# Two pieces of the last batch's rows with three feed-forward pieces, and VectorE and ScalarE bound to the written order in a transformer decoder layer

## The chip, the core and the metric

The kernel runs on one core of a Trainium2 chip. The metric is the device time of one execution in microseconds (us), as the median of three runs. Beside these there is one profiled execution, whose trace is read here. The engines are TensorE (PE; its weight loads are PEld), VectorE (DVE), ScalarE (ACT), GpSimd (POOL) and SyncE (SP), which here issues DMAs.

## The reference

The kernel computes one pre-LayerNorm decoder layer in float32 on x of shape (4, 1024, 256), with a context of shape (4, 64, 256). There are 16 heads of width 16. Cut to what matters:

```python
def layernorm(x): return (x - mean(x)) / sqrt(var(x) + 1e-5)

# self-attention: the energies are not scaled, the softmax is divided by sqrt(256)
q, k, v = split(layernorm(x) @ W_qkv + b_qkv)
attn = softmax(einsum('bqhe,bkhe->bqhk', q, k)) / sqrt(256)
x = x + einsum('bihv,bvhd->bihd', attn, v).reshape(x.shape) @ W_out + b_out

# cross-attention to 64 context tokens for each batch
q = layernorm(x) @ Wq.T + bq; k = ctx @ Wk.T + bk; v = ctx @ Wv.T + bv
x = x + softmax(q k / sqrt(16)) v @ Wo.T + bo

# feed-forward, 256 -> 1024 -> 256; absmean makes ternary weights (-1, 0, 1)
h = gelu(layernorm(x) @ absmean(W_fc).T)            # exact gelu
h = layernorm(h) * ln_w + ln_b
x = x + h @ absmean(W_proj).T
```

`absmean(W)` divides W by the mean of its absolute values, rounds, and clips to one.

## The kernel before, in words

**Phases.** A prologue (to about 66 us) normalises batch 0 and projects its first q and k. The attention loop (66 to 1114 us) follows, then the tail: the last batch's output rows beside the feed-forward of all batches (to 1273 us), and feed-forward alone to the end.

**Attention loop.** There are 16 units: four batches (`b`) of four head groups (`g`), a group being four heads in two pairs. A unit has 16 steps: two halves of 512 query tokens by eight blocks of 128 key tokens. "Step 8.3" here means step 3 of unit 8. A step does the scores of the first pair of heads (`scores`, exponentials on line 848, two tiles of 128x512 on ScalarE), then pieces of other work, then the scores of the second pair, more pieces, and last `weigh`, which multiplies the step before's exponentials by the values on TensorE.

Scores are computed twice. One unit ahead, `maxima` computes them with queries as rows, so that VectorE can reduce each row to its maximum (line 424, two reduces of 128x512 for each pair of score tiles). After the 16 pairs of tiles of a half, lines 430 to 434 negate the maxima and split them into a high and a low part (`nm`, `nm_s`), and lines 436 to 439 turn them with eight small transposes (`mT`). When the unit is reached, a matmul with the selector `sel` adds the negated maxima to the scores in PSUM, so that ScalarE takes the exponential straight from there. The generator `maxima` yields after each pair of tiles, after `nm` and after the turn: 18 yields for half a unit. The loop takes one after the first scores of a step, one after the second, and one more at every fourth step.

**Work between the scores.** Other work is written as generators, cut into pieces at each `yield`: `ln1` (LayerNorm and transposes for the next batch), `project` (q and k, stored to DRAM in `kept_q` and `kept_k`), `values`, `context` (keys and values of the context, lines 444 to 530), `post` (a batch's output projection, second LayerNorm, cross-attention and third statistics, lines 532 to 628), `ternary` (the feed-forward weights) and `bias_row`. They stand in three queues (class `Line`): `due`, `later` and `aside`. Each step adds to a queue's `credit` its pieces left over the steps left to `end`. `fill` (lines 668 to 686) first takes one piece with the tag "free" (it needs no PSUM) from each queue, and then up to `n` pieces of the kind asked for, "rows" (transposes and small work) or "cols" (projections), from the queue with the most credit. The `urgent` queue holds `finish`, which turns and normalises a half's attention output.

A LayerNorm's statistics are `bn_stats` and `bn_aggr` (lines 234 and 235) for each block of 128 tokens. Its reciprocal deviation is a Sqrt on ScalarE (line 240) and a reciprocal on VectorE (line 241); I call these two, with the table loads around the Sqrt, an *rstd group*. The rows are normalised on VectorE (`xn`, line 246) and turned on TensorE (line 60). Right after, GpSimd adds a bias row to the x that was read (`add_row`, line 270). `x_kept` holds a batch's x in DRAM between its attention and its feed-forward.

**What sets the order.** `ordered = tc.keep_in_program_order` pins an instruction to the order in which it is written, among the pinned ones of its engine. TensorE (lines 57 and 60) and the DMAs of SyncE (line 63) are pinned. VectorE, ScalarE and GpSimd are left to a scheduler, which gives each engine its order when the program is built. On the chip each engine runs its own instructions in that order and waits on semaphores for the others. PSUM has one bank for the weighed values (`ps_acc`) and a ring of seven (`ps_ring`) for everything else, so a bank that VectorE or ScalarE has not read yet holds TensorE up.

**Tail.** The feed-forward works on eight halves of batches (512 tokens each). `widen(i)` normalises a half (xn; `xh` and the rest `xl`, lines 259 and 261), multiplies by `wfc` (16 matmuls for each of the four token blocks), takes Gelu (line 955) and statistics of h (lines 958 and 959), then the rstd group, `nmr` (line 963), and normalises h, two blocks on VectorE (line 966) and two on ScalarE (line 969). `narrow(i)` turns h, splits it into `hT` and `hl` (lines 989 and 990), multiplies by `wproj` and adds to x. The places in `WIDE` and `NARROW` give the order of the two. While the last batch's `post` lasts (74 pieces) they alternate with it, decided by `turn`:

```python
    while tag is not None or narrows:
        turn += 1
        if tag is not None and turn % 2:
            exps += "Exp" in tag
            tag = next(last, None)
            continue
```

Of the kernel before, what the change touches and what calls it, by code (L numbers as in the profile page):

```python
# [30 lines left out]
def decoder_layer(ctx, tc, a, out):  # L31
# [21 lines left out]

    ordered = tc.keep_in_program_order
# [7 lines left out]
    def dma(**kwargs):  # L62
        ordered(nc.sync.dma_start(**kwargs))

# [65 lines left out]
    nc.vector.memset(eps_t, LN_EPS)  # L130
# [99 lines left out]
    def ln_stats(pool, mv, blocks):  # L230

        for i, t in blocks:
            st = pool.tile([P, 6], F32, tag="bn", name="bn", bufs=3)
            nc.vector.bn_stats(out=st, in_=xs(t)[:, 0, :])  # L234
            nc.vector.bn_aggr(out=mv[:, i, :], in_=st)

    def ln_rstd(pool, rs, mv):
        n = mv.shape[1]
        sd = pool.tile([P, n], F32, tag="sd", name="sd", bufs=2)
        nc.scalar.activation(sd, mv[:, :, 1], AF.Sqrt, bias=eps_t[:, 0:1])  # L240
        nc.vector.reciprocal(out=rs, in_=sd)

    def ln_normalised(pool, mv, rs, i, t, n):
        xn = pool.tile([P, n, E], F32, tag="xn", name="xn", bufs=2)
        for k in range(n):
            nc.vector.tensor_scalar(  # L246
                xn[:, k, :], xs(t + k)[:, 0, :], mv[:, i + k, 0:1], rs[:, i + k : i + k + 1],
                ALU.subtract, ALU.mult,
            )
        return xn  # L250

    def ln_transposed(dst, xn, rest=None):

        def copy(tokens, r, sides, v):
            to = of_side(dst[:, :, tokens], r, sides)
            nc.scalar.copy(to, v)
            if rest is not None:  # L260
                nc.vector.tensor_tensor(  # L261
                    of_side(rest[:, :, tokens], r, sides), v, to.bitcast(F32), ALU.subtract
                )

        turned_tokens(copy, lambda c, k: xn[:, k, c * P : (c + 1) * P], xn.shape[1])
# [9 lines left out]
    def head_proj(dst, w, bias, g, src, cols):  # L275
        pq = bank()[:, 0 : cols.stop - cols.start]
        product(pq, [(w[:, c, g * P : (g + 1) * P], src[:, c, cols]) for c in range(2)])
        nc.scalar.activation(dst[:, cols], pq, AF.Identity, bias=bias[:, g : g + 1])

    def normalised(dst, acc_sb):  # L280


        views = turned([acc_sb[:, n * P : (n + 1) * P] for n in range(4)])
        n = NG // len(views)
        for side, v in enumerate(views):
            heads = v.rearrange("p t (j e) -> p t j e", e=32)
            r = post_pool.tile([P, 4, n, 1], F32, tag="r", name="r", bufs=3)
            nc.vector.reciprocal(out=r, in_=heads[:, :, :, 0:1])
            nc.vector.tensor_tensor(
                dst[:, :, side * n : (side + 1) * n, :], heads[:, :, :, 1 : 1 + D],  # L290
                r.to_broadcast([P, 4, n, D]), ALU.mult,
            )

    def transposed_blocks(src, n):
        t = post_pool.tile([P, 2, n * P], F32, tag="ao", name="ao")
        turned_tokens(
            lambda tokens, r, sides, v: nc.scalar.copy(of_side(t[:, :, tokens], r, sides), v), src, n
        )
        return t

    def out_proj(ao, k, n, w, t):

        py = bank()
        for i in range(n):
            cols = slice((k + i) * P, (k + i + 1) * P)
            product(py[:, i * E : (i + 1) * E], [(ao[:, c, cols], w[:, c, :]) for c in range(2)])
        nc.vector.tensor_tensor(
            xs(t, n), xs(t, n), py[:, 0 : n * E].rearrange("p (n d) -> p n d", n=n), ALU.add
        )
# [23 lines left out]
    def project(b, c):  # L333
# [6 lines left out]
        for side, half in ((0, 0), (1, 0), (1, 1), (0, 1)):  # L340
# [3 lines left out]
            for i0 in range(0, 512, width):  # L344
# [6 lines left out]
                nc.scalar.activation(hl[:, 0, part].bitcast(F32R), pq, AF.Identity, bias=bias)  # L351
                nc.vector.scalar_tensor_tensor(
# [40 lines left out]
    def values(b):  # L393
        for i in range(NT):
# [4 lines left out]
            nc.vector.tensor_tensor(  # L399
# [4 lines left out]
    def maxima(u):  # L404

        mx = main.tile([P, NT, NG, 2], F32, tag="mx", name="mx", bufs=2)
        m_of[u] = []
        for half in range(2):
# [4 lines left out]
            for t, pair in order:  # L413
                q, k = qk_of[u][pair]
                for kh in range(2):
# [7 lines left out]
                    for n, pm in enumerate(sides):  # L423
                        nc.vector.tensor_reduce(  # L424
                            mx[:, t, 2 * pair + n : 2 * pair + n + 1, kh], pm, AX.X, ALU.max
                        )
                    yield
            sl = slice(half * 4, half * 4 + 4)
            nm = main.tile([P, 4, NG], F32, tag="nm", name="nm", bufs=2)
            nc.vector.tensor_reduce(nm, mx[:, sl, :, :], AX.X, ALU.max, negate=True)  # L430
            by_side = nm.rearrange("p t (a n) -> p t n a", a=2)
            dst = nm_s[:, :, :, 0:2, :]
            nc.vector.tensor_copy(dst[:, :, :, :, 0].bitcast(F32R), by_side)
            nc.vector.tensor_tensor(dst[:, :, :, :, 1], by_side, dst[:, :, :, :, 0], ALU.subtract)
            yield
            views = turned([nm_s[:, n, :, :, :].rearrange("p n a l -> p (n a l)") for n in range(4)])
            mT = main.tile([P, 512], F32R, tag="mT", name="mT", bufs=3)
            for r, v in enumerate(views):
                nc.scalar.copy(mT.rearrange("p (k r i) -> p r k i", r=len(views), k=4)[:, r, :, :], v)  # L439
            m_of[u].append(mT)  # L440
            yield
# [26 lines left out]
    def context():  # L468
# [9 lines left out]
        nc.vector.tensor_reduce(own, ident.rearrange("p (s j i) -> p j s i", s=2, j=4), AX.XY, ALU.add)  # L478
        one = post_pool.tile([P, 32], F32, tag="one", name="one")
        nc.vector.tensor_reduce(one, ident.rearrange("p (s h l) -> p h s l", s=2, l=2), AX.XY, ALU.add)  # L480
        nc.vector.tensor_copy(
            sel_x, one[:, 0:8].rearrange("p (h o) -> p h o", o=1).to_broadcast([P, 8, SK])
        )
        for c in range(2):
# [5 lines left out]
            for j in range(4):  # L490
                nc.vector.tensor_scalar(
# [3 lines left out]
        for b in range(B):  # L495
# [9 lines left out]
            for n in range(2):  # L505
                r = slice(64 * n, 64 * n + 64)
                nc.vector.tensor_tensor(
# [8 lines left out]
    def post(b):  # L516
# [23 lines left out]
        for half in range(2):  # L540
# [14 lines left out]
            for t in range(4):  # L555
# [9 lines left out]
                for s in range(2):  # L565
                    nc.vector.tensor_reduce(  # L566
# [5 lines left out]
            nc.vector.tensor_copy(dst[:, :, :, :, 0].bitcast(F32R), nm)  # L572
            nc.vector.tensor_tensor(dst[:, :, :, :, 1], nm, dst[:, :, :, :, 0], ALU.subtract)
# [3 lines left out]
            for r, v in enumerate(views):  # L577
                nc.scalar.copy(mT.rearrange("p (k r i) -> p r k i", r=len(views), k=4)[:, r, :, :], v)
            att = post_pool.tile([P, 4, NG, NG * D], F32, tag="attx", name="attx")
            before = None  # L580
            for g in range(NG):
# [16 lines left out]
                for p in range(2):  # L598
                    nc.scalar.activation(ex[:, p, :], pe[p], AF.Exp, scale=0.25)
# [11 lines left out]
                nc.scalar.copy(oT, pa)  # L611
# [56 lines left out]
    def fill(kind, n):  # L668

        slots[0] += 1  # L670
        for line in (due, later, aside):
            if line.work and "free" in line.tag and (line is not aside or line.credit >= 1.0):
                line.step(line is aside)
        for least in (0.5, 1.25)[:n]:
# [20 lines left out]
    def ternary(name, *shape):  # L695
# [13 lines left out]
        for i, cols in enumerate(parts):  # L709
            yield "free"  # L710
            nc.vector.tensor_reduce(
# [3 lines left out]
        nc.vector.memset(ones, 1.0)  # L715
# [4 lines left out]
        nc.vector.tensor_reduce(thr[:, 0:1], pt[:, 0 : len(parts)], AX.X, ALU.add)  # L720
        nc.vector.tensor_scalar(thr[:, 0:1], thr[:, 0:1], 1.0 / (P * n), GAMMA_EPS, ALU.mult, ALU.add)
        nc.vector.tensor_scalar(thr[:, 1:2], thr[:, 0:1], -0.5, None, ALU.mult)
        nc.vector.tensor_scalar(thr[:, 0:1], thr[:, 0:1], 0.5, None, ALU.mult)
        for cols in parts:
            yield "free"
            neg = main.tile([P, 512], F32, tag="hl", name="neg", bufs=2)
            nc.vector.tensor_scalar(neg, flat[:, cols], thr[:, 1:2], None, ALU.is_lt)
            nc.vector.scalar_tensor_tensor(
# [4 lines left out]
    def bias_row():  # L733
# [10 lines left out]
        nc.vector.tensor_copy(yrow, pt[:, 0:E])  # L744
# [22 lines left out]
    def weigh(u, half, kb, exps, acc):  # L767
# [11 lines left out]
        nc.scalar.copy(oT, acc)  # L779
# [27 lines left out]
    for pair in range(2):  # L807

        for n in range(2):
            c = 64 * n + 2 * pair  # L810
            for i in range(2):
                nc.vector.tensor_tensor(
                    sel_f[:, pair, :], sel_f[:, pair, :], ident[:, c + i : c + i + 1].to_broadcast([P, P]), ALU.add
                )
    nc.vector.tensor_copy(sel, sel_f)
    add_row(0, bo, NT)
    tops = (None for u in range(NU) for _ in maxima(u))
# [4 lines left out]
    for i in range(18):  # L822
        next(tops)
        if i % 3 != 0 and i < 15:
            due.step()
    due.credit = 0.0
# [5 lines left out]
    def scores(u, half, kb, pair):  # L832
# [14 lines left out]
        for n in range(2):  # L847
            nc.scalar.activation(ex[:, n, :], pe[n], AF.Exp)  # L848
        return ex

    for u in range(NU):
        b, g = divmod(u, NG)
        due.end = later.end = aside.end = 2 * NT * NG * (b + 1)
# [23 lines left out]
        for step in range(2 * NT):  # L877
# [12 lines left out]
            next(tops, None)  # L890
            if urgent:
                fill("rows", 0)
# [5 lines left out]
            for _ in range(1 + (step % 4 == 3) + (u == 0 and step < 3)):  # L898
                next(tops, None)
# [11 lines left out]
    weigh(*pending, acc)  # L911
    while urgent:
# [17 lines left out]
    def widen(i):  # L930
# [14 lines left out]
        for t in range(NH):  # L945
# [9 lines left out]
            nc.scalar.activation(h[:, t, :], ph.rearrange("p a f -> p (a f)"), AF.Gelu)  # L955
            st = ffn.tile([P, 2, 6], F32, tag="bnh", name="bnh", bufs=3)
            for half in range(2):
                nc.vector.bn_stats(out=st[:, half, :], in_=h[:, t, half * 512 : (half + 1) * 512])  # L958
            nc.vector.bn_aggr(out=mv[:, t, :], in_=st)
# [3 lines left out]
        nc.vector.scalar_tensor_tensor(nmr, mv[:, :, 0], -1.0, rs, ALU.mult, ALU.mult)  # L963
        for t in range(0, NH, 2):
            yield ""
            nc.vector.tensor_scalar(
                h[:, t, :], h[:, t, :], mv[:, t, 0:1], rs[:, t : t + 1], ALU.subtract, ALU.mult
            )
            nc.scalar.activation(  # L969
                h[:, t + 1, :], h[:, t + 1, :], AF.Identity, bias=nmr[:, t + 1 : t + 2],  # L970
                scale=rs[:, t + 1 : t + 2],
            )

    def narrow(i):
# [6 lines left out]
        for c in range(HID // P + 2):  # L981
            if c < HID // P:
# [6 lines left out]
                nc.scalar.activation(hT, pt, AF.Copy, scale=w)  # L989
                nc.vector.scalar_tensor_tensor(hl, pt, w, hT.bitcast(F32), ALU.mult, ALU.subtract)  # L990
# [13 lines left out]
        for n in range(2):  # L1004
            rows = xs(t0 + 2 * n, 2)
            nc.vector.tensor_tensor(
# [22 lines left out]

    WIDE, NARROW = (-6, -4, 0, 1, 3, 7, 8, 10, 12), (2, 4, 5, 6, 9, 11, 13, 14, 15)  # L1030
# [5 lines left out]
    while tag is not None or narrows:  # L1036
        turn += 1
        if tag is not None and turn % 2:
# [78 lines left out]
```

## Time and profile before

| | |
|---|---|
| median of three runs | 1395.13 us (1393.49 to 1396.28) |
| the profiled execution, its own time | 1396.0 us |
| its span (first to last instruction) | 1394.2 us, 1.8 us less |
| TensorE busy | 1292.1 us, 93% of the span, 10984 matmuls |
| VectorE busy | 1048.5 us, 75%, 2177 instructions |
| ScalarE busy | 864.0 us, 62%, 1573 instructions |
| GpSimd busy | 81.6 us, 6% |
| mean clock granted to TensorE | 0.964 of full speed |

The reduces of line 424 are VectorE's largest group (639.5 us, 1024 of them), the exponentials of line 848 ScalarE's (544.5 us, 1024 of them). Weighing is the largest part of TensorE's work (279.6 us).

How to read it: a row of the timeline or of the groups has the start and the duration in us, the engine, the line of the kernel, the operation, the tile it writes and the tiles it reads, their shapes, and a count. Square brackets hold the engine's idle time just before and what ended it: `[6.77 <-POOL xwk L452]` says that the engine stood for 6.77 us until GpSimd's instruction of line 452 on tile xwk was done. A busy time counts from an instruction's start to its end, so a TensorE that runs at half clock, or waits inside a chain of matmuls, still counts as busy.

### The profile page before, as it was taken

To read this page: it belongs to the slowest core of one execution; us is meant where nothing else is said; L and a number is where in the kernel's file an instruction comes from. 1 tells how busy PE (TensorE), PEld (TensorE's weight loads), DVE (VectorE), ACT (ScalarE), POOL (GpSimd) and SP (SyncE) were. 2 spreads that over 40 slices of the span, in tenths; PEclk is the share of its full clock that TensorE was granted. 3 is DMA by queue.
4 is the path that set the end of the run, shared out by engine and by line. 5 is a ranking of instruction groups with operands and counts; after the bars stand their busy time and mean duration, and the time that the engine had idled before them with its cause. 6 is when DMAs were issued, how large, how long until landed. Compare 5 with 4: busy or idle time off the path is not lost.

```text
span 1394.2 us, 27597 instructions
## 1 busy us (share of the span) xinstructions
PE 1292.1 (93%) x10984; PEld 721.6 (52%) x10984; DVE 1048.5 (75%) x2177; ACT 864.0 (62%) x1573; POOL 81.6 (6%) x86
## 2 busy tenths in 40 slices
PE   3779999999999999989999999999999989998877
PEld 1334544545454554444545544544445466676767
DVE  5798877777877887788878777878888266565655
ACT  1156666756667677666676676666666846556554
POOL 5021000000100000011000000010000021000100
PEclk9789999999999999989999999999999999999989
DMA  5450312302020211211111202221300010010000
GB/s 155 120 157 31 107 42 81 92 32 77 31 77 1 62 33 29 74 49 41 52 55 38 62 1 86 67 77 46 87 6 1 2 61 1 16 46 16 16 31 31
DMA packets 45841, 72.85 MB, mean 52 GB/s; under 512 B 11025, under 2 KB 27665, under 8 KB 45713
## 3 DMA queue, kind: packets, MB, share of 16 engines
q1 hardware_dynamic: 44448, 68.47, 16.6%
q8 instruction: 87, 1.43, 0.4%
q10 hardware_dynamic: 1072, 2.10, 0.4%
q0 software_dynamic: 192, 0.52, 0.2%
q14 instruction: 42, 0.34, 0.1%
HBM read 46.94 MB, written 24.12 MB: 51 GB/s over the span
## 4 chain that ended last, share of the span: by engine, by line
PE 76%; DVE 16%; ACT 3%; DMA 3%; issue 1%; POOL 1%; SPq 0%; DVEq 0%; POOLq 0%; ACTq 0%
PE ps_ring L57 44%; PE ps_acc L57 16%; PE ps_wide L57 8%; DVE mx L424 8%; PE ps_misc L57 3%; PE ps_ring L60 2%; DVE xn L246 2%; PE ps_misc L60 2%; DMA x<-in_x 1%; DVE nm L566 1%; DVE bn L234 1%; ACT h L955 1%; DMA wk_in<-in_wk 1%; ACT h L969 1%; DVE hl L990 1%
## 5 line engine op out<-in xcount | busy, mean ns | idle before, releaser
L424 DVE TENSOR_REDUCE mx<-ps_ring 128x1 f32<-128x512 f32 x1024 | 639.5, 680 | 117.5 <-PE ps_ring L57 116.5
L848 ACT ACTIVATE exp<-ps_ring 128x512 f32<-128x512 f32 x1024 | 544.5, 603 | 234.7 <-PE ps_ring L57 230.9
L57 PE MATMUL ps_ring<-k,q 64*128 64x512 f32 x1024 | 264.7, 434 | 18.4 <-DMA k<-kept_k 10.9
L57 PE MATMUL ps_acc<-exp,v_sb 128*32 128x512 f32 x2048 | 279.6, 619 | 0.0
L57 PE MATMUL ps_ring<-q,k 64*128 64x512 f32 x1024 | 271.9, 476 | 5.5 <-ACT exp L848 2.6
L57 PE MATMUL ps_ring<-mT,sel 64*128 64x512 f32 x1024 | 227.9, 403 | 0.2 <-ACT mT L439 0.2
L57 PEld LDWEIGHTS ps_ring<-q,k 64*128 64x128 f32 x1024 | 112.2, 187 | 194.5 <-issue 61.2
L57 PEld LDWEIGHTS ps_ring<-k,q 64*128 64x128 f32 x1024 | 126.7, 188 | 106.6 <-ACT exp L848 45.2
L57 PEld LDWEIGHTS ps_ring<-mT,sel 64*128 64x128 f32 x1024 | 107.2, 189 | 6.9 <-ACT mT L439 0.7
L57 PEld LDWEIGHTS ps_acc<-exp,v_sb 128*32 128x32 f32 x2048 | 40.8, 109 | 62.6 <-issue 56.0
L958 DVE BATCH_NORM_STATS2 bnh<-h 128x6 f32<-128x512 f32 x64 | 41.3, 681 | 39.3 <-ACT h L955 39.3
L955 ACT ACTIVATE h<-ps_wide 128x1024 f32<-128x1024 f32 x32 | 32.8, 1026 | 57.6 <-PE ps_wide L57 57.6
L57 PE MATMUL ps_wide<-wproj,hl 128*128 128x256 f32 x256 | 46.8, 306 | 18.4 <-DVE hl L990 18.4
L57 PE MATMUL ps_wide<-wfc,xl 128*128 128x512 f32 x128 | 57.0, 445 | 4.8 <-DVE xl L261 3.3
L246 DVE TENSOR_SCALAR xn<-x,mv,rs 128x256 f32<-128x256 f32 x96 | 55.4, 631 | 6.6 <-PE ps_misc L60 5.6
L990 DVE SCALAR_TENSOR_TENSOR hl<-ps_misc,lnw,hT 128x512 fp32r<-128x512 f32 x64 | 46.3, 730 | 16.9 <-ACT hT L989 16.9
L270 POOL TENSOR_TENSOR x<-x,xbo 128x512 f32<-128x512 f32 x16 | 21.3, 1330 | 559.6 <-DVE xn L246 304.5
L57 PE MATMUL ps_wide<-wfc,xh 128*128 128x512 f32 x128 | 53.7, 420 | 0.0
L989 ACT ACTIVATE hT<-ps_misc,lnw 128x512 fp32r<-128x512 f32 x64 | 42.8, 688 | 16.8 <-PE ps_misc L60 16.8
L351 ACT ACTIVATE hl<-ps_ring,bq_c 128x256 fp32r<-128x256 f32 (+1 forms) x30 | 14.7, 490 | 54.8 <-PE ps_ring L57 50.5
L57 PEld LDWEIGHTS ps_wide<-wproj,hl 128*128 128x128 f32 x256 | 35.3, 194 | 23.6 <-DVE hl L990 20.9
L234 DVE BATCH_NORM_STATS2 bn<-x 128x6 f32<-128x256 f32 x96 | 38.9, 416 | 10.2 <-DMA x<-in_x 8.6
(161 smaller groups left out, 1452.2 us busy)
## 6 DMA issues: line engine op xcount, KB each, us to landing
k<-kept_k SPq DMA_DIRECT2D x248, 64.0 KB
q<-kept_q SPq DMA_DIRECT2D x240, 64.0 KB
kept_q<-hl SPq DMA_DIRECT2D x15, 512.0 KB
kept_k<-hl SPq DMA_DIRECT2D x14, 512.0 KB
out<-x SPq DMA_DIRECT2D x16, 256.0 KB
x<-in_x SPq DMA_DIRECT2D x3, 1024.0 KB
x_kept<-x SPq DMA_DIRECT2D x3, 1024.0 KB
x<-x_kept SPq DMA_DIRECT2D x3, 1024.0 KB
```

The source lines that it names most:

```text
L57: ordered(nc.tensor.matmul(*args, **kwargs))
L60: ordered(nc.tensor.transpose(*args))
L234: nc.vector.bn_stats(out=st, in_=xs(t)[:, 0, :])
L246: nc.vector.tensor_scalar(xn[:, k, :], xs(t + k)[:, 0, :], mv[:, i + k, 0:1], rs[:, i + k : i + k + 1], ALU.subtract, ALU.mult,)
L270: nc.gpsimd.tensor_tensor(xs(t, 2), xs(t, 2), row.rearrange("p (o d) -> p o d", o=1).to_broadcast([P, 2, E]), ALU.add,)
L351: nc.scalar.activation(hl[:, 0, part].bitcast(F32R), pq, AF.Identity, bias=bias)
L424: nc.vector.tensor_reduce(mx[:, t, 2 * pair + n : 2 * pair + n + 1, kh], pm, AX.X, ALU.max)
L848: nc.scalar.activation(ex[:, n, :], pe[n], AF.Exp)
L955: nc.scalar.activation(h[:, t, :], ph.rearrange("p a f -> p (a f)"), AF.Gelu)
L958: nc.vector.bn_stats(out=st[:, half, :], in_=h[:, t, half * 512 : (half + 1) * 512])
L989: nc.scalar.activation(hT, pt, AF.Copy, scale=w)
L990: nc.vector.scalar_tensor_tensor(hl, pt, w, hT.bitcast(F32), ALU.mult, ALU.subtract)
```

## The change

It has six parts.

1. A thin wrapper `Engine` around VectorE and ScalarE pins every instruction while its flag `fixed` is set. The flag is set from the attention loop's first scores until after its last `weigh`, so there both engines run in the written order.
2. In the tail, single instructions are pinned: the copy to `xh` and the subtraction for `xl`, the pair that normalises h, and the pair `hT` and `hl`. The rest of the tail stays with the scheduler.
3. The end of `maxima` becomes a generator of its own, `turn_maxima`. The loop now takes two pairs of maxima every step, none at a fourth place; `nm` is written right after a half's last pair, and the turn takes the next step's "rows" slot, where `urgent` work otherwise stands. In those two cases a "rows" piece may still go first, if `later` has a credit of 1.5 (`behind`).
4. The queue `later` ends two steps sooner.
5. In `fill`, a queue that has given a free piece counts as having been served in this slot.
6. In the tail, of five turns two go to `post` and three to the feed-forward, where they took one each.

```diff
+    class Engine:
+        def __init__(self, engine):
+            self.engine, self.fixed = engine, False
+        def __getattr__(self, name):
+            op = getattr(self.engine, name)
+            def call(*args, **kwargs):
+                done = op(*args, **kwargs)
+                if self.fixed:
+                    ordered(done)
+                return done
+            return call
+    vector, scalar = Engine(nc.vector), Engine(nc.scalar)
...
     def maxima(u):
...
+                    if kh == 1 and (t, pair) == order[-1]:
+                        turning.append(turn_maxima(u, mx[:, half * 4 : half * 4 + 4, :, :]))
                     yield
-            sl = slice(half * 4, half * 4 + 4)
-            nm = main.tile([P, 4, NG], F32, tag="nm", name="nm", bufs=2)
...
+    def turn_maxima(u, mx):
+        nm = main.tile([P, 4, NG], F32, tag="nm", name="nm", bufs=2)
+        vector.tensor_reduce(nm, mx, AX.X, ALU.max, negate=True)
...
             if line.work and "free" in line.tag and (line is not aside or line.credit >= 1.0):
                 line.step(line is aside)
+                line.slot = slots[0]
...
+    def top():
+        next(tops, None)
+        if turning and turning[-1] not in begun:
+            next(turning[-1])
+            begun[turning[-1]] = slots[0]
...
-    for i in range(18):
-        next(tops)
+    for i in range(16):
+        top()
...
+    run(turning.popleft())
...
+    vector.fixed = scalar.fixed = True
     for u in range(NU):
         b, g = divmod(u, NG)
-        due.end = later.end = aside.end = 2 * NT * NG * (b + 1)
+        due.end = aside.end = 2 * NT * NG * (b + 1)
+        later.end = due.end - 2
...
             exps = [scores(u, half, kb, 0)]
-            next(tops, None)
-            if urgent:
-                fill("rows", 0)
+            top()
+            behind = 1 if later.credit >= 1.5 else 0
+            if turning and begun[turning[0]] < slots[0]:
+                fill("rows", behind)
+                run(turning.popleft())
+            elif urgent:
+                fill("rows", behind)
                 urgent.popleft()()
             else:
                 fill("rows", 1)
             exps.append(scores(u, half, kb, 1))
-            for _ in range(1 + (step % 4 == 3) + (u == 0 and step < 3)):
-                next(tops, None)
+            for _ in range(2 if u == 0 and step < 3 else 1):
+                top()
...
     weigh(*pending, acc)
+    vector.fixed = scalar.fixed = False
...
-            nc.scalar.copy(to, v)
+            copied = scalar.copy(to, v)
             if rest is not None:
-                nc.vector.tensor_tensor(
+                ordered(copied)
+                ordered(vector.tensor_tensor(
                     of_side(rest[:, :, tokens], r, sides), v, to.bitcast(F32), ALU.subtract
...
-        if tag is not None and turn % 2:
+        if tag is not None and turn % 5 in (0, 2):
             exps += "Exp" in tag
             tag = next(last, None)
             continue
```

The pinned pairs for h and for `hT` and `hl` are written as that for `xh` and `xl`.

## Prediction

> **What bounds it now.** I read the page first: engines' busy time, then the chain that ended last.
>
> ```profile
> PE 1292.1 (93%) x10984; PEld 721.6 (52%) x10984; DVE 1048.5 (75%) x2177; ACT 864.0 (62%) x1573; POOL 81.6 (6%) x86
> PE 76%; DVE 16%; ACT 3%; DMA 3%; issue 1%; POOL 1%; SPq 0%; DVEq 0%; POOLq 0%; ACTq 0%
> ```
>
> TensorE bounds; a gain can only be a wait of TensorE that goes. Next the table by stretches (start:end, length, busy PE, PEld, DVE, ACT, POOL, granted clock): attention loop, FFN beside the last `post`, FFN alone, then two pairs inside one tail round.
>
> ```profile
> 65.90:1113.70 1047.80, 1014.16 (x9207) 512.91 (x9208) 829.11 (x1732) 697.59 (x1351) 36.11 (x41) 0.98 0.19 54
> 1123.00:1273.00 150.00, 137.72 (x800) 100.62 (x800) 95.09 (x203) 87.33 (x119) 18.21 (x14) 0.97 0.09 27
> 1273.00:1394.20 121.20, 97.57 (x632) 87.62 (x632) 75.87 (x139) 67.28 (x85) 6.62 (x5) 0.91 0.07 22
> 1328.90:1334.00 5.10, 5.06 (x16) 4.38 (x17) 1.28 (x2) 0.51 (x1) 0.00 (x0) 0.51 0.25 84
> 1334.00:1345.00 11.00, 11.00 (x72) 9.53 (x71) 7.43 (x14) 6.19 (x8) 0.00 (x0) 1.00 0.03 10
> 1353.90:1358.00 4.10, 4.10 (x15) 3.57 (x16) 1.28 (x2) 0.45 (x1) 0.00 (x0) 0.58 0.18 57
> ```
>
> A busy PE hides stalls, so I priced the loop by steps from the timeline (time between successive first exps). A bare step (eight score matmuls, two pairs of maxima, a weighing) takes 2.9 us; a piece of eight projection matmuls adds 0.87; a piece of transposes 0.52; `kx,q` 0.82, `mTx` 0.77, `ex,vx` 0.97. For 255 steps: 255x2.9 + 154x0.87 + 116x0.52 + 24x0.82 + 24x0.77 + 12x0.97 = 984. They took 1045.7, so 61 us is excess: unit 0 15.3, unit 4 5.8, unit 8 17.2, unit 12 8.7, units 13 to 15 11.2, the rest 3. That is what the loop can lose. Unit 0's, in the timeline:
>
> ```profile
> 93.08 5.52 DVE L246 TENSOR_SCALAR xn<-x,mv,rs 128x256 f32<-128x256 f32 x8
> 98.68 1.26 POOL L270 TENSOR_TENSOR x<-x,bo 128x512 f32<-128x512 f32 x1 [0.23 <-DVE xn L246]
> 99.89 1.48 POOL L452 COPY xwk<-xwk_in 128x64 f32<-128x64 f32 x8
> 100.18 2.10 PE L57 MATMUL ps_ring<-ctx_in,xwk 128*32 128x256 f32 x16 [6.77 <-POOL xwk L452]
> ```
>
> GpSimd did batch 1's `bo` adds (they wait on xn) ahead of casting xwk, and TensorE stood 6.77 us. Unit 8 has a load instead, and each of the loop's eight rstd groups takes ScalarE from the exps:
>
> ```profile
> 586.02 0.39 SPq L63 DMA_DIRECT2D x<-in_x  x1
> 592.16 0.75 DVE L234 BATCH_NORM_STATS2 bn<-x 128x6 f32<-128x256 f32 x2 [0.23 <-DMA x<-in_x]
> 375.98 1.28 ACT L240 ACT_TABLE_LOAD   x1
> 377.27 0.30 ACT L240 ACTIVATE sd<-mv,eps_t 128x8 f32<-128x8 f32 x1
> 377.59 1.28 ACT L848 ACT_TABLE_LOAD   x1
> ```
>
> Last, the chain through one round of the FFN-only tail (start, us, piece); the next half's xn stand ahead of this half's rstd and normalising on VectorE:
>
> ```profile
> 1321.50 2.27 DVE xn L246 x4
> 1323.77 0.10 DVE rsh L241
> 1323.89 1.25 DVE nmr L963
> 1325.16 2.37 ACT h L969 x2
> 1327.53 0.58 ACT hT L989
> 1328.14 0.76 DVE hl L990
> 1328.94 3.36 PE ps_wide L57 x11
> ```
>
> TensorE waits 5.3 us from 1323.6 to 1328.9, then runs 5.1 us at clock 0.51: 2.5 us more.
>
> **Loop: what the order changes.** The two programs' written orders, compared by engine, show that nearly everything reading PSUM already ran in it: 63 of 1445 VectorE and 35 of 1340 ScalarE instructions of the loop come later than written. So binding moves mainly what reads no PSUM: statistics, Sqrt and its two table loads, reciprocals, xn. The groups move from steps (unit.step) 0.6, 4.12, 8.0, 8.3, 8.12, 12.0 and 12.12 to 2.12 (batch 1's ln1 comes off unit 0), 4.14, 8.0, 8.2, 8.14, 12.0 and 12.14, and one Sqrt at 0.10 stands where the scheduler had shared a load: table loads go from 42 to 43.
>
> Unit 0: on GpSimd the casts now come before the `bo` adds, so the 6.8 us wait goes, and about 3 us of the half-clock time behind it. The rstd group pushed into unit 2 costs there what the groups at 4.12, 8.12 and 12.12 cost: excesses of 5.7, 5.1, 5.2. By hand, in the new order, such a group costs 0.65 + 0.75 ahead of it and about 3.0 held by Sqrt (1.28 + 0.30 + 1.28 above): 4.4 to 4.7. Net -6.8 - 3 + 4.7 = **-5**; bounds: -10 (the new group hidden) to 0 (late next are the casts' own loads: xwq's cast at 102.4 us still waited 1.03 for its DMA). Those three groups: 3x(4.7 - 5.7) = **-3**, bounds -9 to +9.
>
> Unit ends 8 and 12: VectorE must now do a block's statistics (0.39 + 0.16 = 0.56 each, six of them 3.4 us) and the rstd ahead of the reduces that free the ring's banks; queued behind are the maxima, and TensorE waits for their bank. At 8.0 the statistics also wait for the load: issued at 586.0, landed 592.1, needed 2 to 4.4 us earlier in the new order. About 15 against 12 us at unit 8, 5 against 3.5 at 12: **+4.5**, bounds -2 to +16 (load wait and statistics fully exposed, both ends). SP is pinned in both programs, so the x_kept store (581.6 to 586.0) and this load keep their places.
>
> Ternary pieces (units 13 to 15): their 0.5-and-over VectorE work falls behind a step's reduces, not between them, and a line waits a slot after a free piece: 11.2 to about 6, **-5**, bounds -9 to +4. Maxima: two pairs each step in place of a third one every fourth step; a pair adds 0.51 of TensorE and 1.23 of VectorE and the count is the same (992 matmuls), nm and turn a slot apart: **0**, bounds -5 to +5; cover is that VectorE has 0.79 of the loop's time, and without it each of 32 turns would add up to 0.5. `later.end - 2`: three xwo pieces move from behind the loop into it, 3x0.87 = 2.6 and back: 0. Engine wrapper: 0. Loop **-8.5**.
>
> **Tail.** The ratio of post to FFN pieces goes from 1:1 to 2:3, post's 74 pieces last longer, and when they end 22 of 32 widening groups and 32 of 64 narrowing groups are out, not 16 and 24. A bare round took 27.3 us (1295.7, 1323.0, 1350.3) for 19.2 of TensorE's own; one with post beside it loses nothing like 8. So 1 to 1.5 rounds less of 5.3 + 2.5: 1.25x7.8 = **-10**, bounds -16 to 0. Post's first 33 us (1123 on) hold 10 us of waits for att, wo and xn; three FFN pieces between cover some: **-4**, bounds -10 to +4 (more post latency at the end). The pinned xh/xl, h and hT/hl pairs already run in that order but for 7 hl: 0. One more table load, 1.28: **+1.3**. Tail **-12.7**.
>
> On the clock: the rows show 0.51 after a wait of 5.3 us and 0.58 after one of about 3.2, and I assume that the rounds which stay bare keep both. [...]
>
> On the loads: the rows show the Sqrt at 377.27, 0.01 us after its load ended, so I take 1.28 a load. [...]
>
> **Sum.** 1396.0 (span 1394.2 + 1.8) - 8.5 - 12.7 = 1374.8; the median of the runs shown stands 0.9 below the profiled execution: **1374**. The terms' half-widths, 5, 9, 9, 6.5, 5, 8 and 7, taken as independent, make 19; four fifths of that, 16 each way, is this case's own range: 1358 to 1390.
>
> **Rivals.** (1) *Slower: blocked queues.* Eight groups, forecast near 5 each, expose all: 4x1.12 of statistics, 2.9 of Sqrt and loads, 2.6 of half clock = 10. Full price 8x5 = +40: 1414; the sign turns where eight groups eat the 21.2 (2.65 each) and the 2.8 of a visible loss (0.35): 3 us more per group, 8 in all. So 1398 to 1414. For: an in-order queue holds exps behind a Sqrt that waits for statistics. Against: before already runs those pieces between exps at about 5. Chance 0.20. (2) *Loop unmoved*, only the tail gains: 1382; for, the 63 and 35 above. 0.13. (3) *Most excess goes*, 61 to 25, tail -15: 1344; for, scheduler-placed pieces lie in most of it. 0.15. (4) *Nothing moves*, both orders end equal: 1395. 0.06. Forecast 0.46.
>
> **Chances.** 0.2% (2.8 us) is what a measurement of this kernel can tell. Faster: 0.46 + 0.13 + 0.15 less 0.03 for the forecast's edge: 0.71; same 0.09; slower 0.20. The range leaves out about 0.1 on each side: below 1350 two thirds of rival 3, above 1406 half of rival 1.
>
> **To look for.** In after: no wait of 6.8 on xwk near 100 us; unit 2 longer by 4 to 5 and unit 0 shorter by 10; unit 8's end near 15; VectorE's reduces late by at most 1.2 per statistics piece; three bare rounds or fewer in the tail. Wrong if the loop's excess is above 65, or the tail from the loop's end is not shorter by 8.

## The result and the profile after

The changed kernel takes 1419.32 us (1413.62 to 1420.83, four runs) against 1395.51 for the kernel before in the same comparison: 23.8 us slower, a ratio of 1.0165 with a 95% interval of 1.0134 to 1.0197. The forecast was 1374, its own range 1358 to 1390; the chances were reckoned with limits of 1350 and 1406. The measured time lies above all of them.

I cut each profiled execution into three: up to the first exp of the loop; the loop, from there to the first exp of its last step; and the tail, from there to the end.

| kernel | span | first exp at | loop | tail | median of its runs |
|---|---|---|---|---|---|
| before | 1394.2 | 65.9 | 1045.7 | 282.6 | 1395.5 |
| after | 1418.8 | 64.5 | 1067.9 | 286.4 | 1419.3 |

So the loop lost 22.2 us and the tail 3.8. By the prediction's step prices the loop's own work is 2.6 more (three xwo pieces moved in) and its excess over them rose from about 61 to about 81. Both signs of being wrong that the prediction named have come: an excess above 65, and a tail that is not 8 shorter.

The page of the changed kernel, engines and chain. TensorE's line 57 is now 58, SyncE's 63 is 64, and everything that goes through the wrapper has line 76:

```profile
PE 1307.1 (92%) x10984; PEld 729.6 (51%) x10984; DVE 1060.2 (75%) x2177; ACT 865.6 (61%) x1574; POOL 80.8 (6%) x86
PE 68%; DVE 20%; ACT 5%; DMA 3%; SPq 2%; issue 1%; POOL 1%; DVEq 0%; ACTq 0%; POOLq 0%
```

The same instructions ran (one more on ScalarE, the table load), but TensorE's share of the chain fell from 76% to 68%, and VectorE, ScalarE and SyncE's queue took it over. The table by stretches (loop, feed-forward beside `post`, feed-forward alone; columns as in the prediction):

```profile
64.50:1134.50 1070.00, 1031.48 (x9252) 519.88 (x9254) 842.07 (x1736) 697.67 (x1351) 35.69 (x41) 0.97 0.19 54
1143.70:1333.70 190.00, 167.08 (x952) 128.26 (x953) 116.17 (x236) 107.21 (x141) 18.46 (x14) 0.93 0.06 20
1333.70:1418.80 85.10, 69.32 (x481) 62.90 (x479) 56.71 (x103) 48.99 (x63) 5.21 (x4) 0.95 0.08 26
```

The stretch beside `post` grew by 40 us and the bare one shrank by 36, as the ratio is meant to do. The clock beside `post` fell from 0.97 to 0.93, though, which speaks for waits in it that were not there (behind the one of 6.26 us shown below it was 0.50, from 1245.2 to 1250). Now the loop's places. Unit 0, from the timeline:

```profile
93.47 0.38 SPq L64 DMA_DIRECT2D kept_k<-hl  x1
96.26 0.47 ACT L76 ACTIVATE hl<-ps_ring,bq_c 128x256 fp32r<-128x256 f32 x1 [8.85 <-DMA kept_k<-hl]
96.63 2.05 ACT L76 ACTIVATE exp<-ps_ring 128x512 f32<-128x512 f32 x4
97.28 0.97 PE L58 MATMUL ps_ring<-k,q 64*128 64x512 f32 x2 [7.56 <-ACT exp L76]
99.88 1.93 PE L58 MATMUL ps_ring<-ctx_in,xwk 128*32 128x256 f32 x16
```

The last line has no bracket any more: the wait for xwk is gone, as forecast. But three lines up ScalarE stands 8.85 us before a copy into an `hl` tile, whose buffer a store of k is still to read. That store was issued only at 93.47, behind fetches of q and k and small loads that had kept SyncE's queue busy since 62. The exps are ready behind the copy: TensorE had done their scores by 89.72 (97.28 less the 7.56 it then stands for them). They start at 96.63, behind it, and that the copy is first comes from the binding. The end of unit 7 and the start of unit 8:

```profile
587.09 1.28 ACT L76 ACT_TABLE_LOAD   x1
588.08 0.42 DVE L76 BATCH_NORM_STATS2 bn<-x 128x6 f32<-128x256 f32 x1
591.16 0.39 SPq L64 DMA_DIRECT2D x<-in_x  x1
591.39 0.30 ACT L76 ACTIVATE sd<-mv,eps_t 128x8 f32<-128x8 f32 x1 [3.01 <-DVE mv L76]
591.71 1.28 ACT L76 ACT_TABLE_LOAD   x1
592.53 0.79 PE L58 MATMUL ps_ring<-k,q 64*128 64x512 f32 x1 [3.82 <-DVE mx L76]
593.00 2.06 ACT L76 ACTIVATE exp<-ps_ring 128x512 f32<-128x512 f32 x4
597.25 0.43 DVE L76 BATCH_NORM_STATS2 bn<-x 128x6 f32<-128x256 f32 x1 [4.17 <-DMA x<-in_x]
```

`flush` wrote the batch's last three statistics pieces in one row. VectorE does them ahead of the reduces, from 588.08 to 591.35; ScalarE has loaded the Sqrt's table and waits 3.01 us for them, and TensorE waits 3.82 for a bank. Then VectorE stands 4.17 us for a load of x with reduces ready behind it. Unit 13 shows the same with the raw weights:

```profile
965.18 0.69 DVE L76 TENSOR_REDUCE part<-raw 128x1 f32<-128x512 f32 x1 [3.56 <-DMA raw<-in_wfc]
968.61 1.09 ACT L76 ACTIVATE exp<-ps_ring 128x512 f32<-128x512 f32 x2 [3.93 <-PE ps_ring L58]
```

Behind the waits of units 0, 7 and 8 TensorE runs at a granted clock of 0.50 to 0.60 (the value after the five busy times):

```profile
97.20:105.00 7.80, 7.72 (x46) 3.78 (x46) 6.08 (x14) 3.31 (x9) 1.50 (x8) 0.59 0.51 178
592.50:600.00 7.50, 5.29 (x26) 2.48 (x28) 3.22 (x9) 4.22 (x8) 0.00 (x0) 0.50 0.83 232
599.00:607.00 8.00, 7.30 (x47) 3.66 (x49) 7.73 (x23) 2.83 (x5) 0.00 (x0) 0.60 0.52 140
```

The tail, beside `post`:

```profile
1240.33 1.26 POOL L291 TENSOR_TENSOR x<-x,yrow 128x512 f32<-128x512 f32 x1 [0.23 <-DVE rsh L76]
1240.37 1.24 DVE L76 SCALAR_TENSOR_TENSOR nmr<-mvh,rsh 128x4 f32<-128x4 f32 x1
1241.64 2.37 ACT L76 ACTIVATE h<-h,nmr,rsh 128x1024 f32<-128x1024 f32 x2 [2.45 <-DVE nmr L76]
1243.92 1.05 ACT L76 CAST xh<-ps_misc 128x512 fp32r<-128x512 f32 x2
1245.27 0.79 PE L58 MATMUL ps_wide<-wfc,xl 128*128 128x512 f32 x1 [6.26 <-DVE xl L76]
```

The cast to xh, whose rows TensorE had turned by 1238.1, stands behind the normalising of h, which waits for its rstd; TensorE waits 6.26 us for xl.

### The profile page after: what moved, and what is told of

The parts are those of the page before. It is cut to its first block, busy times and chain, and to the rows that moved or that the text cites. A ratio compares the mean times of both kernels' runs of the same rounds, so it can differ in the third digit from the quotient of the medians.

```text
span 1418.8 us, 27562 instructions
## 1 busy us (share of the span) xinstructions
PE 1307.1 (92%) x10984; PEld 729.6 (51%) x10984; DVE 1060.2 (75%) x2177; ACT 865.6 (61%) x1574; POOL 80.8 (6%) x86
## 4 chain that ended last, share of the span: by engine, by line
PE 68%; DVE 20%; ACT 5%; DMA 3%; SPq 2%; issue 1%; POOL 1%; DVEq 0%; ACTq 0%; POOLq 0%
PE ps_ring L58 38%; PE ps_acc L58 14%; DVE mx L76 9%; PE ps_wide L58 8%; PE ps_misc L58 3%; DVE xn L76 3%; PE ps_misc L61 2%; PE ps_ring L61 2%; DVE nm L76 2%; SPq L64 2%; ACT exp L76 2%; DVE bn L76 1%; DMA x<-in_x 1%; ACT h L76 1%; DVE hl L76 1%
## 5 line engine op out<-in xcount | busy, mean ns | idle before, releaser
L76 DVE TENSOR_REDUCE mx<-ps_ring 128x1 f32<-128x512 f32 x1024 | 646.2, 682 | 116.8 <-PE ps_ring L58 116.2
L58 PE MATMUL ps_ring<-k,q 64*128 64x512 f32 x1024 | 272.0, 431 | 34.1 <-DMA k<-kept_k 10.8
L58 PE MATMUL ps_ring<-q,k 64*128 64x512 f32 x1024 | 283.2, 479 | 6.7 <-DVE hl L76 3.0
L58 PE MATMUL ps_ring<-mT,sel 64*128 64x512 f32 x1024 | 236.3, 405 | 0.4 <-ACT mT L76 0.4
L58 PEld LDWEIGHTS ps_ring<-q,k 64*128 64x128 f32 x1024 | 117.3, 187 | 202.1 <-issue 52.5
L58 PEld LDWEIGHTS ps_ring<-k,q 64*128 64x128 f32 x1024 | 130.2, 189 | 119.5 <-ACT exp L76 45.4
L58 PEld LDWEIGHTS ps_ring<-mT,sel 64*128 64x128 f32 x1024 | 110.4, 189 | 6.0 <-ACT mT L76 0.7
L76 DVE BATCH_NORM_STATS2 bn<-x 128x6 f32<-128x256 f32 x96 | 38.3, 405 | 11.2 <-DMA x<-in_x 11.1
```

What stands on the lines that cost most here:

```text
L58: ordered(nc.tensor.matmul(*args, **kwargs))
L76: done = op(*args, **kwargs)
```

## The experiments

Theory Q: the binding costs, by instructions that wait for something late (a DMA, a burst of statistics) and hold ready exps and reduces behind them. Its rival M: the new places of the maxima and the credits cost, binding is neutral. For the tail there are two questions. Of the ratio, T: the waits only move from the bare rounds to those beside `post`; its rival is the forecast. Of the pins, P: they cost what the ratio gains; its rival is that they are neutral.

### Binding alone, and everything but the loop's binding

`bind_only` is the kernel before with this:

```diff
+    vector.fixed = scalar.fixed = True        # from the first scores
...
+    vector.fixed = scalar.fixed = False       # after the loop's last weigh
```

> The kernel before with one thing added: VectorE and ScalarE bound to the written order in the attention loop (maxima, turns, queue ends and the tail as before). Theory Q (bound queues): in the changed kernel ScalarE stood 8.9 us in front of a copy to hl whose buffer a store from kept_k still read, 3.0 and 3.4 us with the Sqrt's table loaded and the exps behind it at the ends of units 7 and 11, and VectorE 4.2 us for the load of x and 3.6 us for the load of raw; all of these come from binding alone. So about 1410 to 1418, the loop about 1060 to 1070 us. Theory M (the maxima's new places and the credits cost it, binding is neutral): 1393 to 1398, loop about 1046.

Measured: 1427.37 us, ratio 1.0232 (1.0208 to 1.0256), loop 1077.8: 32.1 more than before; the time is 9 above the upper end of Q. The 7.5 us at step 0.5, 5.6 each at 7.15 and 11.15, 5.1 at 8.1 and 3.2 at 13.5 are there without the other parts. `unbound` is the changed kernel without the flag:

```diff
-    vector.fixed = scalar.fixed = True
```

> The changed kernel with the flag for VectorE and ScalarE never set in the loop, all else as changed. Theory Q: the loop falls from 1068 to about 1046 (its excess over the step prices from 81 to about 61), the time to about 1396 to 1400. Theory M: 1414 to 1420.

Measured: 1386.47, ratio to before 0.9943 (0.9926 to 0.9959), loop 1034.5. So binding costs 33.4 us of loop on the new order (1067.9) and 32.1 on the old one; M falls. Each loop time is that of one profiled execution: `tail_back` below, whose loop is the changed kernel's, took 1060.5 for it, and `free` and `xh_free`, whose loop is that of `unbound`, took 1036.5 and 1036.6. So by the profiles the price on the new order is 24 to 33 us; the medians, by their ratios of 1.0165 and 0.9943, give 31. The loop's other changes gain 11.2 (9.1 in `xh_free`), and 13.7 of excess, which neither theory expected.

### Which engine

```diff
-    vector.fixed = scalar.fixed = True
+    vector.fixed = True          # vector_only;  scalar.fixed = True in scalar_only
```

> The changed kernel with only VectorE bound in the loop. Binding both costs 33 us of loop (1034.5 to 1067.9). Theory Q gives VectorE the wait for the load of x (4.2 and its followers, about 9 in unit 8), that for raw (5.5 in unit 13) and half of the two unit ends: 12 to 20, so the loop at 1047 to 1055 and 1398 to 1407 in all. If one engine alone does it, the loop stays at about 1035 or rises to 1065.

> The changed kernel with only ScalarE bound in the loop. Theory Q gives ScalarE the copy to hl in unit 0 (7.5) and the Sqrt with its table loaded ahead of the exps at the ends of units 7 and 11 and in units 2, 4, 8 and 12 (about 10): 12 to 20, so the loop at 1047 to 1055 and 1398 to 1407. If one engine alone does it, about 1035 or 1065.

Measured: VectorE alone 1413.37 (ratio 1.0133, 1.0109 to 1.0158), loop 1059.2, 24.7 above unbound. ScalarE alone 1388.53 (0.9951, 0.9933 to 0.9968), loop 1039.4, 4.9 above. My even split was wrong: VectorE costs five times as much. By units, `vector_only` is above `unbound` mainly in unit 8 (9.9 us), unit 12 (5.8) and unit 2 (5.2), which hold the waiting load of x and, by the prediction's list, six of the loop's rstd groups. In unit 0 both engines stand in one place (total, times, longest; `vector_only` first, then `scalar_only`):

```profile
DVE hl L76 <- ACT hl L76: 50.1, 41, 8.3
```

```profile
ACT hl L76 <- DMA kept_k<-hl: 7.0, 1, 7.0
```

The late store blocks either engine, since VectorE's half of the `hl` split waits for ScalarE's copy. But unit 0 is not dearer for it: it took 72.5 and 71.9 us, against 73.0 in `unbound`, where TensorE waits 2.8 us for xwk and ScalarE 4.91 for a Sqrt's statistics. In the changed kernel it took 76.1, and 72.5 in `tail_back`. So the 8.85 us show what is late at the head of the queue; of binding's price unit 0 holds 3 us or nothing.

### The waits taken away at their source

`bound_later` keeps both engines bound and everything else of the changed kernel, with three edits (and 12 pieces counted for each `ternary`, not 10):

```diff
             next(loading, None)
+            if (u, step) == (8, 3):           # not at step 8.0
+                due.add(ln1(3), 2); due.add(project(3, 0), 8); due.add(values(3), 8)
...
         dma(out=flat..., in_=a[name]...)      # ternary: raw
+        yield "free"
+        yield "free"
...
-                dma(out=t[r : r + 32, :], in_=src[s, q, :, 1 : 1 + D, :])             # xbk, xbq
+                nc.gpsimd.dma_start(out=t[r : r + 32, :], in_=src[s, q, :, 1 : 1 + D, :])
```

> The changed kernel, both engines bound, with three waits of the queues taken away at their source and nothing else: batch 3's ln1 and projections join the queue at step 8.3, not 8.0 (the load of x has landed by then); the first reduce of raw comes two pieces after its DMA is issued; the eight small loads of xbk and xbq go by GpSimd's queue, so that SyncE reaches the store which frees hl about 5 us sooner. Theory Q (those waits, each in front of a bound queue, are the price): unit 8 falls by about 8 us (from 78.3), unit 13 by about 5 (from 68.6), unit 0 by 3 to 5 (from 76.1), in all 1400 to 1406. If binding costs through the order of the reduces and exps as such, the units stay as they are and the time stays at 1415 to 1421.

Measured: 1405.0 (1403.14 to 1407.44). Unit 8 fell from 78.3 to 69.4, unit 13 from 68.6 to 64.5, unit 0 from 76.1 to 69.5; the rest stayed within 1.1. That is what Q said for units 8 and 13 and in all. In unit 0 it is more than the 3 to 5 expected, and not all of it is binding's price: `tail_back` was at 72.5 there without any of the edits. The row of unit 0 kept half of its wait:

```profile
90.85 0.38 SPq L64 DMA_DIRECT2D kept_k<-hl  x1
93.66 0.47 ACT L76 ACTIVATE hl<-ps_ring,bq_c 128x256 fp32r<-128x256 f32 x1 [4.05 <-DMA kept_k<-hl]
```

`bound_post72` spreads the burst at the unit's end:

```diff
-    POST = 64
+    POST = 72
```

> The changed kernel with 72 instead of 64 pieces counted for post, so that the last three statistics pieces and the Sqrt of a batch are no longer flushed together at the unit's end (they come at steps 7.10 to 7.14 and 11.10 to 11.14). Theory Q: the 5.1 us at step 7.15 and the 4.6 at 11.15 go and 2 to 3 come back at 7.14 and 11.14, and x_kept's store and so the load of x come a step sooner: units 7, 8, 11 and 12 together fall by 6 to 12 (from 286.5), the time to 1407 to 1413. If only the count of statistics matters, nothing moves: 1416 to 1421.

Measured: 1402.53 (1401.04 to 1404.85). Units 7, 8, 11 and 12 together went from 286.5 to 274.3, 12.2 less, at the upper end of Q, and the time is 4.5 us below Q's lower end; units 13 and 14 gave 4.9 back. The tail got 6.9 shorter (286.4 to 279.5), which I had not expected; the last batch's statistics and its Sqrt are now written before the loop's end, but I did not test that this is why.

### The tail's ratio and its pins

`tail_only` is the kernel before with the ratio alone; `tail_back` is the changed kernel with the ratio undone:

```diff
-        if tag is not None and turn % 2:
+        if tag is not None and turn % 5 in (0, 2):
```

> The kernel before with two post pieces to three feed-forward in the tail, nothing else. Theory T (the waits of a feed-forward round, 3 to 6 us from xn to the first matmul that needs xl or hl, only move from the bare rounds to the rounds beside post): 1394 to 1400. The forecast on record (bare rounds cost, rounds beside post do not): about 1384, 11 less than before.

> The changed kernel with the tail's pieces one to one again. Theory T: 1413 to 1420, the tail after the loop's last exp within 4 us of the changed kernel's 286. The forecast on record: about 1431, 12 more than the changed kernel.

Measured: `tail_only` 1385.83 (ratio 0.9932, 0.9917 to 0.9947), tail 271.8, 10.8 less than before. T falls here, and the forecast's term holds. But `tail_back` took 1413.42 (1407.78 to 1415.34), less than the changed kernel, tail 280.8 against 286.4. So in the changed kernel the ratio gains nothing, where the forecast said 12, and something beside it takes the gain. `pins_only` adds the tail's pins to `tail_only`; `free` takes them out of `unbound`:

```diff
-                ordered(copied)
-                ordered(vector.tensor_tensor(          # xl
+                vector.tensor_tensor(
...                                                      # so too for h, and for hT and hl
```

> The kernel before with two post pieces to three and the tail's pins, the loop untouched. Theory P: 1394 to 1400, 8 to 14 above the kernel with the ratio alone (1385.8), with a wait of about 6 us for xl in the tail. Pins neutral: 1384 to 1388.

> The changed kernel without both bindings: the flag never set in the loop, and xh/xl, the normalising of h and hT/hl in the tail not pinned; the new maxima, queue ends and the tail's ratio stay. Theory P (pinning in the tail costs what the ratio gains: with the pins ScalarE holds the cast to xh behind the normalising of h, and TensorE waits 6.3 us for xl): the tail falls from 282 in the kernel without the loop's binding to about 270, the time to 1373 to 1377. If the pins are neutral: 1385 to 1388.

Measured: `pins_only` 1396.81 (ratio 1.002, 1.0006 to 1.0034), tail 284.8: 13.0 above the ratio alone (11.0 in the medians). `free` 1371.10 (0.983, 0.9806 to 0.9855), tail 268.0: 14.1 below `unbound` (15.4 in the medians). P holds both ways. TensorE's waits for xl in the tail, of `tail_only` first and then of `pins_only`, show where (total, times, longest):

```profile
PE ps_wide L57 <- DVE xl L261: 2.9, 1, 2.9
```

```profile
PE ps_wide L57 <- DVE xl L262: 12.4, 3, 6.3
```

Which pin: `xh_free` drops only that of xh and xl.

> The changed kernel unbound in the loop, with h's and hT/hl's pins in the tail but without that of xh and xl. Theory P1 (the cast to xh is held behind the normalising of h on ScalarE, because both are pinned): the 6.3 and 3.3 us waits for xl go and the tail falls from 282 to 270 to 273, the time to 1373 to 1377. If the pins of h, hT and hl cost as much by themselves (the wait of 4.9 for hl): 1380 to 1387.

Measured: 1376.06 (0.9852, 0.9823 to 0.9881), tail 272.6. That one pin takes 9.5 of the 14.1, as P1 said. In its timeline the casts to xh stand ahead of h again, and no wait of 6 us for xl is left:

```profile
1203.13 0.59 ACT L76 CAST xh<-ps_misc 128x512 fp32r<-128x512 f32 x1 [1.18 <-PE ps_misc L61]
1205.24 0.57 ACT L76 CAST xh<-ps_misc 128x512 fp32r<-128x512 f32 x1
1207.80 2.38 ACT L76 ACTIVATE h<-h,nmr,rsh 128x1024 f32<-128x1024 f32 x2 [1.51 <-DVE nmr L76]
```

### What remains of binding, and the fastest version

`bound_all` has the three edits of `bound_later`, 72 pieces and no tail pins; `free_all` is the same with nothing bound.

> Both engines bound in the loop, without the tail's pins, with all four waits moved away (batch 3's ln1 from step 8.3, raw's reduces later, xbk and xbq by GpSimd's queue, 72 pieces for post). If the four waits were all of the price, the loop is within 5 us of the same kernel unbound, and the time is 1370 to 1376. If binding has a price of its own (reduces and exps held behind the statistics of units 2, 4, 8 and 12), 10 us or more remain: 1378 to 1386.

> The same kernel with nothing bound in the loop. The moved work helps a scheduler less, since it put the exps and reduces ahead of such waits already: at most 8.2's 5 us of the load and 2 or 3 at 0.6, so 1362 to 1370. If the moves are worth nothing unbound: 1369 to 1372.

Measured: 1375.62 (1370.25 to 1379.13) and 1369.21 (1365.34 to 1375.48); loops 1046.1 and 1031.5. Binding still costs 14.6 us in the two profiled executions and 6.4 in the medians, whose ranges overlap. The profiled execution of `bound_all` was its slowest (1379.13) and that of `free_all` nearly its fastest (1366.29), so 14.6 is a high figure. The expectation's two cases are not told apart: the time lies in the first, the loop in the second. By the profiles the four waits were about 19 of the 33, by the medians about 25 of 31. By units, `bound_all` is above `free_all` mainly in unit 14 (6.1 us), units 2 and 7 (3.8 each) and unit 11 (2.7). Part of it is seen at step 14.6, 4.4 us over its price, in the chain of waits of `bound_all`:

```profile
1012.61 1.28 DVE mx L76 x2
1013.89 2.25 DVE xn L76 x4
1016.14 0.40 DVE neg L76
1016.57 1.65 DVE wfc L76
1018.22 0.61 DVE mx L76
1018.87 1.27 PE ps_ring L58 x5
```

Here nothing is late: 4.3 us of VectorE work that reads no PSUM is written in one row, and TensorE waits 1.9 us for the reduce behind it. In the kernel before, in the order of its scheduler, the reads of raw stand between reduces in shorter rows (1.26 us at 1025.27, 0.68 at 1026.78).

Two trials on `free`. `free_pool` binds GpSimd instead, so that the casts of xwk come ahead of the `bo` adds; `free_post72` counts 72 pieces.

> The kernel without any of the new pins (1371.1) with one engine bound instead, GpSimd, in the loop: the casts of xwk then come ahead of batch 1's bo adds. If TensorE's wait for xwk (8.5 us over the step price at 0.6) goes as the forecast assumed and nothing takes its place: unit 0 falls by 6 to 9 to about 65, and the time to 1363 to 1366. If hl's wait for its store or the casts' own load stands behind it, as it does in the changed kernel: unit 0 falls by less than 3, 1369 to 1373.

> The kernel without any of the new pins with 72 pieces counted for post. With a scheduler free to put the statistics between the reduces the flush at units 7 and 11 costs 2.1 and 1.2, so at most 3 to 5 is to be had there, and up to 5 of the load of x at 8.2: 1364 to 1371. If the queues do not matter where nothing is bound: 1370 to 1373.

Measured: `free_pool` 1367.18 (ratio to before 0.9792, 0.9772 to 0.9813), `free_post72` 1369.87 (0.9814, 0.9795 to 0.9833), which is no clear gain over `free`. In `free_pool` the wait for xwk (2.7 us in `free`) is gone, but one of 4.7 for kx stands in its place, and unit 0 fell by 0.6 us only (72.7 to 72.1): steps 0.6 and 0.7 stayed 4.7 and 3.3 over their prices. That is the second case of the expectation, though the time is 1.8 below it. The other 3 to 4 us lie in several places within what such runs differ by, and I can't assign them. By its median it is the fastest version measured, 28.9 us under the kernel before in the same comparison.

## Why the prediction was wrong

**The step that failed is the cost of binding.** From the comparison of the written orders I concluded that few instructions move (63 of 1445, 35 of 1340) and summed small terms to -8.5. The count was not the price. What costs is what stands first when an input is late, and I had looked for that only at the rstd groups and the load of x. Measured, binding is +33.4 on the new order by the profiles (+31 by the medians); I had put it, with all else in the loop, at -8.5.

**Unit 0, -5 forecast.** The wait for xwk went, but unit 0 took 76.1 in place of 75.4 (72.5 in `tail_back`), and unit 2 got its group (4.2 us over its price; 4.7 forecast). What was late next was not in my list: the store on SyncE that frees `hl`. I had said that SyncE's order is pinned in both programs and so costs nothing, and had not followed who now waits in line for one of its transfers. `free_pool`, where the wait for kx took the place of that for xwk, speaks against the 6.8 having been there to gain whole.

**The three mv2 groups, -3 forecast.** At units 4, 8 and 12 they cost 5.2, 6.8 and 5.8 in place of 5.7, 5.1 and 5.2: +1.8, inside the bounds, of the other sign. The sum also took 5.7 for all three; with its own three excesses it gives -1.9.

**Unit ends 8 and 12, +4.5 forecast.** From step 7.15 to 8.3 the excess is 15.5 against 12.0, and from 11.15 to 12.1 5.2 against 3.5: +5.2. This term held.

**Ternary, -5 forecast.** Units 13 to 15 went from 11.2 to 13.4. I had bounded VectorE's work there and forgotten its DMA: the first reduce is written one slot after the load, and stood 3.56 us for it with reduces behind.

**Maxima, 0 forecast.** With nothing bound the new loop has 12 to 14 us less excess. That is outside my bounds of 5. Which of its parts does it (two pairs every step, the turn's slot, the queue that ends sooner) was not taken apart.

**Tail.** The ratio's terms were -10 for the rounds, -4 for the first 33 us and +1.3 for a table load; alone the ratio measured -10.8 in the profile's tail and -9.0 in the medians (1394.8 to 1385.8): near the sum of -12.7. Its three terms were not measured one by one. The pins were put at 0 because the pairs already ran in that order but for 7 `hl`. They cost 13 to 14 in the profiles, 11 to 15 in the medians. This is the second step that failed: I had compared each pair with itself; the pins also order the pairs among each other, xh behind h.

**The rivals.** Rival 1 had the sign and the mechanism, a queue blocked at its head. Its place and price were wrong: it priced eight rstd groups at 10 us each and ended at 1414; the four that stand apart (units 2, 4, 8 and 12) cost 4 to 7, nearer the forecast's 4.4 to 4.7. The blocks that decided were two loads, two bursts at unit ends and VectorE's own rows, and a store for 3 us or less. The loads of tables took the 1.28 that the forecast counted: in the rows of unit 7 above the second load starts at 591.71, 0.02 us after the Sqrt's end, and takes 1.28, and the exps resume at 593.00, 0.01 us after it.

## What to carry to other kernels

Before an engine is bound to a written order, go through what it reads and writes that can be late: for each DMA-fed operand, each buffer that a store must free, each burst of pieces, ask what stands ready behind it. A comparison of two orders shows what moves, not what is late; here the scheduler's freedom was worth most where a few instructions wait. And pins on separate pairs are also pins between the pairs.

## What the runs showed of the hardware

The 128x4 operation that makes nmr on VectorE takes 0.16 us by itself, and 1.24 us in the lines shown above, where GpSimd's 128x512 add began 0.04 us before it: the two ended within 0.02 us of each other. All four such cases in the two kernels (two of eight in each) took 1.24, each with 1.22 us of overlap, and one with 0.71 of overlap took 0.73. By these figures nothing of such an nmr was done on VectorE until GpSimd's add was over. In the tail that is 1.1 us on the chain each time.

The other is TensorE's clock behind a wait. In the changed kernel it was 0.50 behind a wait of 2.92 us; the first line is a timeline row, the second a row of the table by stretches:

```profile
1291.73 1.01 PE L58 MATMUL ps_wide<-wproj,hl 128*128 128x256 f32 x3 [2.92 <-DVE hl L76]
```

```profile
1291.70:1294.50 2.80, 2.77 (x12) 1.99 (x16) 1.38 (x2) 1.43 (x3) 0.00 (x0) 0.50 0.02 6
```

The wait that the prediction put at about 3.2 us, before 1353.90 in the kernel before, is 2.98 in the timeline, and the clock behind it was 0.61 (1353.9 to 1356). But the length alone does not decide. In `free` and `free_pool` the same four matmuls, behind the same work, waited the same 2.72 us, and the clock was 0.50 behind the first wait and 1.00 behind the second:

```profile
1251.80 1.22 PE L58 MATMUL ps_wide<-wproj,hl 128*128 128x256 f32 x4 [2.72 <-DVE hl L76]
1251.80:1254.10 2.30, 2.30 (x12) 1.98 (x16) 1.32 (x3) 1.61 (x3) 0.00 (x0) 0.50 0.03 7
```

```profile
1245.65 0.74 PE L58 MATMUL ps_wide<-wproj,hl 128*128 128x256 f32 x4 [2.72 <-DVE hl L76]
1245.70:1248.00 2.30, 2.30 (x18) 1.34 (x19) 1.32 (x3) 1.64 (x4) 0.00 (x0) 1.00 0.03 7
```

Another of these matmuls waited 3.49 us in `free` (before 1147.26) and 3.48 in `free_pool` (before 1143.55), and there too the clock was 0.50 in the first and 1.00 in the second. So no one length between 2.72 and 3.48 us separates the waits that cost the clock from those that do not, and what does is not shown. The length of a wait by itself was no ground to forecast the clock from.
